# Layer 1 of a two-layer metaformer: rows' denominators inverted on ScalarE, five convolution taps on TensorE instead of seven, centred x kept in PSUM

## The chip, the cores and the metric

The kernel runs on one core of a Trainium2 chip. Its engines are named as in the profile: PE is TensorE (PEld its weight loads), DVE VectorE, ACT ScalarE, POOL GpSimd, SP the engine that issues the DMAs. Each works through its own queue of instructions strictly in order and waits by semaphores for the others. The metric is the device time of one execution in microseconds; lower is better.

## The reference, cut to what matters

The input x is 2 images of 96 channels by 96 x 96 pixels, fp32. Layer 0 (a selective-scan block and a feed-forward block) takes most of the time and isn't touched. Layer 1 is:

```python
    x = x + _L1_conv_ref(_ln_c(x), kv_w, q_w, lepe_w, lepe_b, proj_w, proj_b)
    t = _to_tokens(x)
    t = t + _L1_ffn_ref(_ln_t(t), W1, b1, W2, b2)
    x = _from_tokens(t, x)
...
def _ln_c(v, eps=1e-6):                       # over the 96 channels
    m = jnp.mean(v, axis=1, keepdims=True)
    s = jnp.var(v, axis=1, keepdims=True)
    return (v - m) / jnp.sqrt(s + eps)
...
def _L1_conv_ref(x, kv_w, q_w, lepe_w, lepe_b, proj_w, proj_b):
    k, v = jnp.split(kv, 2, axis=2)           # kv = kv_w x, three heads of 32
    x_samp = x.reshape(B, C, hh, R, ww, R).mean(axis=(3, 5))      # cells of 2 x 2 pixels
    q_samp = ...                              # q_w x_samp
    lepe = lax.conv_general_dilated(v, lepe_w, (1, 1), [(2, 2), (2, 2)],
                                    feature_group_count=C)        # 5 x 5, each channel alone
    attn = jax.nn.softmax(k^T q_samp * scale, axis=-2)
    distribution = v attn                     # 96 channels on 48 x 48 cells
    samp_unfold = unfold3(x_samp)             # each cell's 3 x 3 neighbours
    dmat = jax.nn.softmax(x_unfold . samp_unfold * C ** -0.5, axis=-1)
    feature = dmat . unfold3(distribution)    # each pixel: nine neighbouring cells, weighted
    out = feature + lepe
    return proj_w out + proj_b
```

(The einsums are written short here.) The feed-forward block is 96 to 384 to 96 with ReLU, its products in fp8 and its sums rounded to fp16. Its own norm is `_ln_t`, over the channels too, with eps 1e-5.

## The kernel before

The work is laid out with channels on partitions and pixels along the free dimension. A stripe is 6 rows of pixels, T = 576 columns; most instructions work on half of one, H2 = 288 columns.

Layer 1 goes through the two images one after the other, each in three stages.

1. **The norm for k, q, v** (`_l1_before`), 16 stripes. For each half stripe: PE multiplies x by (I - mean) into a PSUM tile `pc` (L1107), so `pc` is the centred x. ACT squares it into `sq` (L1112) and copies it to `xc` in SBUF (L1113). PE averages the squares into PSUM tile `va` (L1116). ACT turns that into 1/sqrt(va + eps) in place, as Ln (L780) and Exp with scale -0.5 (L781), in `_power`. DVE multiplies `xc` by `va` into `xn` (L1120). Then come the products with the weights of k, v and q, and their copies from PSUM on ACT.
2. **Attention** (`_l1_attention`): all pixels against all cells. It isn't touched. DVE adds the exponentials up there (L1425), PE makes scores (L1351) and weighted values (L1412).
3. **Rows** (`_l1_turn`, then `_l1_rows` for 8 groups of 12 pixel rows). For each group:
   - four matmuls and ACT copies bring v with a border of two pixels into `vch` (L1519, L1522);
   - `near`, three times: PE makes scores with the neighbouring cells (`st`, L1543), ACT takes Exp (L1547), POOL multiplies by a mask (L1549), PE sums the weights into `pd` and the weighted distribution into `po` (L1557), DVE inverts `pd` into `rd` (L1563) and multiplies `rd` by `po` into `ft` (L1564). All of these are 384 columns wide;
   - the 5 x 5 convolution: 25 taps. The taps listed in `ON_PE`, seven of them, are folded into the projection: PE multiplies a shifted view of `vch` by a projection matrix whose rows are scaled by the tap's weights (L1595; these matrices, `W.pt`, are built once ahead of layer 1). The other 18 are one DVE instruction each over 1152 columns that adds to `acc` (L1576 for the first, L1579 for the rest);
   - `project`: one PSUM tile `pp` for each half stripe gathers the taps on PE, then `ft` (L1599), then `acc` (L1605); DVE adds the bias and x (L1608);
   - `_plan_ffn`, the feed-forward block, which layer 0 uses as well: the norm once more (L794 centred, L799 Square, L800 copy to `xc`, L803 mean, `_power`, L807 the product as fp8), the hidden layer (L818, L821, L825, L828), the second product (L837, L841, L845) and the residual on POOL (L846).

What sets the order: the code of stages 1 and 3 only records operations, each with its engine, a cost, the tiles it reads and writes, and a due time. `_Plan.order` then places them one by one. It knows for every engine when it is free, for every tile how many buffers there are, and adds a fixed lag when one engine hands over to another; the earliest possible operation goes next, ties by due time. The order so found is fixed for each engine, so a DVE instruction that waits holds everything behind it in DVE's queue. PSUM is one pool of 8 buffers with a single tag, from which `pc`, `va`, `st`, `pd`, `po`, `pp`, the hidden layer and everything else in a stage take theirs. A buffer is free again after its tile's last user. A line of `_l1_rows` shows the form of a record, with the cost as a number of columns:

```python
        op("dve", 2200, lambda: nc.vector.reciprocal(rd.ap, pd.ap[:C, :384]), (pd,), (rd,))
        op("dve", 384, lambda: nc.vector.tensor_tensor(
            ft.ap[:, i], rd.ap, po.ap[:C, :384], ALU.mult), (rd, po), ((ft, i),))
```

The functions that the change touches:

Of the kernel before, what the change touches and what calls it, by code (L numbers as in the profile page):

```python
# [11 lines left out]
F8 = mybir.dt.float8e5  # L12
AF = mybir.ActivationFunctionType
ALU = mybir.AluOpType
# [11 lines left out]
C = 96  # L26
# [5 lines left out]
T = WIN * HW  # L32
H2 = T // 2
# [68 lines left out]
class _Plan:  # L102
# [15 lines left out]
    def op(self, eng, cost, run, r=(), w=(), due=0.0, tab=None, also=()):  # L118
        o = _Op(eng, cost, run, due, tab)
        ref = lambda t: t if isinstance(t, tuple) else (t, None)  # L120
        meets = lambda a, b: a is None or b is None or a == b
        for t, key in map(ref, r):
            o.deps.update(p for p, q in t.writes if meets(key, q))
        for t, key in map(ref, w):
            o.deps.update(p for p, q in t.writes + t.reads if meets(key, q))
        for t, key in map(ref, r):
            t.reads.append((o, key))
        for t, key in map(ref, w):
            t.writes.append((o, key))
        o.deps.discard(o)  # L130
        for t in [x[0] for x in map(ref, list(r) + list(w))] + list(also):
            if t not in o.tiles:
                o.tiles.append(t)
        for t in o.tiles:
            if not t.users and t.tag != "p":
                t.queue.append(t)
            t.users.append(o)
        self.ops.append(o)
        return o
# [632 lines left out]
        sofar += o.cost  # L772


def _power(k, op, v, eps):

    v_ = lambda: v.ap[:C, :H2]

    def run():
        k.nc.scalar.activation(v_(), v_(), AF.Ln, bias=eps[:C])  # L780
        k.nc.scalar.activation(v_(), v_(), AF.Exp, scale=-0.5)  # L781

    op("act", H2, run, (), (v,), tab="e", times=2)


def _plan_ffn(k, S, op, ps, temp, pool, bufs, ffn, x1):

    nc = k.nc
    cols = lambda c: slice(c * H2, (c + 1) * H2)
    xc, s1, xq = temp("fxc"), temp("fsq"), S.tile(pool, [C, T], "fxq", bufs, F8)  # L790
    for c in range(2):
        def norm(c=c):
            pc, va = ps("fxc"), ps("fva")
            op("pe", H2, lambda: nc.tensor.matmul(  # L794
                pc.ap[:C, :H2], k.less_mean, x1.ap[:, cols(c)], start=True, stop=True),
                (x1,), (pc,), (xc,))

            def centred():
                nc.scalar.activation(s1.ap[:, cols(c)], pc.ap[:C, :H2], AF.Square)  # L799
                nc.scalar.copy(xc.ap[:, cols(c)], pc.ap[:C, :H2])  # L800

            op("act", H2, centred, (pc,), ((xc, c), (s1, c)), times=2)
            op("pe", H2, lambda: nc.tensor.matmul(  # L803
                va.ap[:C, :H2], k.mean96, s1.ap[:, cols(c)], start=True, stop=True),
                ((s1, c),), (va,), (xq,))
            _power(k, op, va, k.eps5)
            op("dve", H2, lambda: nc.vector.tensor_tensor(  # L807
                xq.ap[:, cols(c)], xc.ap[:, cols(c)], va.ap[:C, :H2], ALU.mult, saturate=False),
                ((xc, c), va), ((xq, c),))

        norm()
    h16 = S.tile(pool, [128, NM, T], "fh16", bufs, HP)
    h8 = S.tile(pool, [128, NM, T], "fh8", bufs, F8)
    for m in range(NM):
        for c in range(2):
            def hidden(m=m, c=c):
                ph = ps("fph")
                op("pe", H2 // 2, lambda: nc.tensor.matmul(  # L818
                    ph.ap[:, :H2], ffn.w1[:, m * 128 : (m + 1) * 128], xq.ap[:, cols(c)],
                    start=True, stop=True), ((xq, c),), (ph,), (h16,))  # L820
                op("act", H2, lambda: nc.scalar.copy(h16.ap[:, m, cols(c)], ph.ap[:, :H2]),  # L821
                   (ph,), ((h16, m),))

            hidden()
        op("act", T, lambda m=m: nc.scalar.activation(  # L825
            h16.ap[:, m, :], h16.ap[:, m, :], AF.Relu, bias=ffn.b1[:, m : m + 1]),
            (), ((h16, m),))
        op("act", T, lambda m=m: nc.scalar.activation(  # L828
            h8.ap[:, m], h16.ap[:, m], AF.Copy, saturate=False), ((h16, m),), ((h8, m),))
    y16, x2 = S.tile(pool, [C, T], "fy16", bufs, HP), temp("x2")  # L830
    for c in range(2):
        def last(c=c):
            py = ps("fpy")

            def run():
                for m in range(NM):
                    nc.tensor.matmul(py.ap[:C, :H2], ffn.w2[:, m, :], h8.ap[:, m, cols(c)],  # L837
                                     start=(m == 0), stop=(m == NM - 1))

            op("pe", 3 * H2 // 2, run, (h8,), (py,), (y16,))  # L840
            op("act", H2, lambda: nc.scalar.copy(y16.ap[:, cols(c)], py.ap[:C, :H2]),  # L841
               (py,), ((y16, c),))

        last()
    op("act", T, lambda: nc.scalar.activation(y16.ap, y16.ap, AF.Identity, bias=ffn.b2), (), (y16,))  # L845
    op("pool", T, lambda: nc.gpsimd.tensor_tensor(x2.ap, x1.ap, y16.ap, ALU.add), (x1, y16), (x2,))  # L846
    return x2
# [242 lines left out]
def _l1_before(k, P, S, W, M, x2d):  # L1090


    nc = k.nc
    op = _op(S)
    ps = lambda name: S.tile(P.ps, [128, 512], "p", 8, name=name)
    cols = lambda c: slice(c * H2, (c + 1) * H2)
# [1 line left out]
    xn, xs, kH, qH, vT, mk, mq = map(held, ("xn", "xs", "kH", "qH", "vT", "mk", "mq"))  # L1098

    def stripe(s):  # L1100
        xt, xc, sq = (S.tile(P.wk, [C, T], n, 3, name="n" + n) for n in ("xt", "xc", "sq"))
        S.op("sp", 1.0, lambda: nc.sync.dma_start(xt.ap, x2d[:, s * T : (s + 1) * T]), (), (xt,))
        here = lambda c: slice(s * T + c * H2, s * T + (c + 1) * H2)

        def norm(c):
            pc, va = ps("nxc"), ps("nva")
            op("pe", H2, lambda: nc.tensor.matmul(  # L1107
                pc.ap[:C, :H2], k.less_mean, xt.ap[:, cols(c)], start=True, stop=True),
                (xt,), (pc,), (xc,))

            def centred():
                nc.scalar.activation(sq.ap[:, cols(c)], pc.ap[:C, :H2], AF.Square)  # L1112
                nc.scalar.copy(xc.ap[:, cols(c)], pc.ap[:C, :H2])  # L1113

            op("act", H2, centred, (pc,), ((xc, c), (sq, c)), times=2)
            op("pe", H2, lambda: nc.tensor.matmul(  # L1116
                va.ap[:C, :H2], k.mean96, sq.ap[:, cols(c)], start=True, stop=True),
                ((sq, c),), (va,))
            _power(k, op, va, k.eps6)
            op("dve", H2, lambda: nc.vector.tensor_tensor(  # L1120
                xn.ap[:, here(c)], xc.ap[:, cols(c)], va.ap[:C, :H2], ALU.mult),
                ((xc, c), va), ((xn, s),))
            pk = ps("pk")
            op("pe", H2, lambda: nc.tensor.matmul(  # L1124
                pk.ap[:C, :H2], W.k, xn.ap[:, here(c)], start=True, stop=True),
                ((xn, s),), (pk,))
            op("act", H2, lambda: nc.scalar.copy(kH.ap[:C, here(c)], pk.ap[:C, :H2]),
               (pk,), ((kH, s),))

        for c in range(2):  # L1130
            norm(c)
        for n, f in enumerate((ALU.max, ALU.min)):
            op("dve", T, lambda n=n, f=f: nc.vector.tensor_reduce(
                mk.ap[:, n, s : s + 1], kH.ap[:C, s * T : (s + 1) * T], AX.X, f),
                ((kH, s),), ((mk, (n, s)),))
        hs = S.tile(P.wk, [C, WIN, CELLS], "hs", 2)
        cells = lambda: xs.ap[:, 1 + 3 * s : 4 + 3 * s, 1 : CELLS + 1]

        def pairs():
            v = xn.ap[:, s * T : (s + 1) * T].rearrange("p (i w t) -> p i w t", w=CELLS, t=2)  # L1140
            nc.gpsimd.tensor_tensor(hs.ap, v[:, :, :, 0], v[:, :, :, 1], ALU.add)

        op("pool", H2, pairs, ((xn, s),), (hs,))
        op("pool", H2 // 2, lambda: nc.gpsimd.tensor_tensor(
            cells(), hs.ap[:, 0:6:2], hs.ap[:, 1:6:2], ALU.add), (hs,), ((xs, s),))
        op("pool", H2 // 2, lambda: nc.gpsimd.tensor_scalar(cells(), cells(), 0.25, None, ALU.mult),
           (), ((xs, s),))
# [336 lines left out]


NEAR = 2 * (CELLS + 2)
ON_PE = tuple(range(7))


def _l1_rows(k, P, S, W, ffn, M, distT, x2, out, q, at):  # L1490
# [43 lines left out]
    def near(i):  # L1534
# [25 lines left out]

        sums(pd, lambda t: k.ones[:NEAR])
        sums(po, lambda t: distT.ap[:NEAR, j + t])
        op("dve", 2200, lambda: nc.vector.reciprocal(rd.ap, pd.ap[:C, :384]), (pd,), (rd,))  # L1563
        op("dve", 384, lambda: nc.vector.tensor_tensor(  # L1564
            ft.ap[:, i], rd.ap, po.ap[:C, :384], ALU.mult), (rd, po), ((ft, i),))

# [17 lines left out]
    def project(c2):  # L1584
# [26 lines left out]

        for c in range(2):
            part(c)
        y = _plan_ffn(k, S, op, ps, temp, P.wk, 3, ffn, x3)
        row = q * R + c2 * WIN
        S.op("sp", 1.0, lambda: nc.sync.dma_start(
            out[:, row : row + WIN, :].rearrange("c r w -> c (r w)"), y.ap), (y,), ())
# [227 lines left out]
```

## Time and profile before

| | us |
|---|---|
| median of 3 runs | 9094.67 |
| lowest, highest | 9091.53, 9099.18 |
| layer 0 and the loading of layer 1's weights | about 6923 |
| norm for k, q, v, first and second image | 78 and 81 |
| attention, first and second image | 628 and 626 |
| rows, first and second image | 379 and 379 |

Over the whole span, PE is busy 7530.7 us (83%), DVE 8172.0 (90%), ACT 6380.3 (70%) and POOL 6182.8 (68%). These are averages over stages with different limits; the change lies in about a tenth of the span, so it is the stages' own busy times that count. In the views below, a line such as "rd<-pd 96x384 f32" means that tile `rd` was written from tile `pd`, 96 partitions by 384 elements. PE's fp32 products are two matmul instructions each in the profile.

### The profile page before, as it was taken

The page shows a single profiled execution, that of the slowest core. Times are in us where ns is not written, and L with a number is a line of the kernel's source. Part 1 is how long each engine was busy: PE and PEld are TensorE (multiplying, and loading weights), DVE is VectorE, ACT ScalarE, POOL GpSimd, SP SyncE. Part 2 cuts the span into 40 slices and gives each one's busy share as a digit, 9 for nine tenths or more (in the row PEclk, how much of TensorE's full clock was granted, in tenths as well). Part 3 has the DMA queues.
Part 4 walks back from the last instruction along what each step waited for, and adds up shares of the span by engine and source line. Part 5 has one row for each costly group of instructions (what it writes and reads, how often), then busy time and mean ns, then how long its engine had stood idle before and what let it go on. Part 6 is the DMA issues. An engine that isn't in the chain of part 4 may idle for free. (4 is left out here: it accounts for less than half of the span.)

```text
span 9094.2 us, 122612 instructions
## 1 busy us (share of the span) xinstructions
PE 7530.7 (83%) x43793; PEld 3599.2 (40%) x43793; DVE 8172.0 (90%) x5681; ACT 6380.3 (70%) x10752; POOL 6182.8 (68%) x3931
## 2 busy tenths in 40 slices
PE   6888888888788888888887888887857999989998
PEld 3333344443334344444343443343423334543345
DVE  2999999999999999999999999999996998959988
ACT  4677777777777777777777777777745785677755
POOL 4988888888888888888888988888863001310022
PEclk8889889898888888889898889888857999989999
DMA  2444444444444444444444444444431000000000
GB/s 81 134 145 140 140 143 140 139 139 140 139 138 142 139 143 143 138 139 145 138 137 141 141 136 143 144 136 144 142 122 36 2 2 7 23 25 2 3 11 21
DMA packets 335681, 969.61 MB, mean 107 GB/s; under 512 B 50424, under 2 KB 52144, under 8 KB 334768
## 3 DMA queue, kind: packets, MB, share of 16 engines
q1 hardware_dynamic: 335056, 961.64, 33.3%
q8 instruction: 348, 5.70, 0.3%
q14 instruction: 277, 2.27, 0.1%
HBM read 788.04 MB, written 132.17 MB: 101 GB/s over the span
## 5 line engine op out<-in xcount | busy, mean ns | idle before, releaser
L1018 POOL TENSOR_TENSOR h<-h,cre 128x864 f32<-128x864 f32 x2048 | 4121.7, 2021 | 824.2 <-DVE h L1015 405.4
L1015 DVE TENSOR_TENSOR_SCAN h<-dA,bp 128x864 f32<-128x864 f32 x2048 | 4001.7, 1954 | 250.3 <-DVE bp L1005 5.7
L991 ACT ACTIVATE dA<-dlr,A 128x576 f32<-128x576 f32 x3072 | 2156.9, 765 | 1223.4 <-DVE h L1015 1138.3
L1005 DVE TENSOR_TENSOR bp<-dur,B 128x864 f32<-128x864 f32 x2048 | 2176.4, 1063 | 249.1 <-DMA dur<-du_d 42.3
L1028 PE MATMUL y<-h,fold 128*32 128x288 f32 (+2 forms) x18432 | 1875.3, 453 | 111.0 <-POOL h L1018 107.7
L1002 PE MATMUL B<-bt,selb 128*128 128x288 bf16 x2048 | 637.8, 313 | 1105.7 <-DVE bp L1005 1098.1
L536 PE MATMUL pc<-xin,off 96*96 96x288 f32 x4608 | 1328.7, 416 | 0.9 <-ACT xin L501 0.9
L1028 PEld LDWEIGHTS y<-h,fold 128*32 128x32 f32 x18432 | 765.4, 120 | 1370.2 <-issue 647.8
L1355 ACT ACTIVATE pr<-sc 128x960 f32<-128x960 f32 (+1 forms) x1080 | 955.0, 936 | 257.9 <-DVE sums L1425 145.6
L1425 DVE TENSOR_TENSOR sums<-sums,pr 128x1920 f32<-128x1920 f32 (+1 forms) x510 | 1059.5, 2077 | 59.1 <-ACT pr L1355 7.0
L536 PEld LDWEIGHTS pc<-xin,off 96*96 96x96 f32 x4608 | 710.9, 165 | 622.7 <-issue 381.1
L1506 POOL MEMSET vch<- 96x32 f32 x16 | 2.0, 124 | 1328.6 <-DVE dist L1384 1266.2
L1351 PE MATMUL sc<-qH,kH 32*128 32x480 f32 (+1 forms) x3240 | 709.6, 602 | 10.1 <-DMA q<-qH 10.1
L1351 PE MATMUL sc<-q,kH 32*128 32x480 f32 (+1 forms) x1080 | 564.5, 602 | 0.0
L1412 PE MATMUL av<-pr,vT 128*32 128x480 f32 (+1 forms) x4320 | 533.5, 565 | 3.8 <-ACT av L1429 3.5
L1002 PEld LDWEIGHTS <-selb 128*128 128x128 bf16 x2048 | 201.6, 100 | 711.8 <-issue 636.6
L1351 PEld LDWEIGHTS sc<-qH,kH 32*128 32x128 f32 x3240 | 285.3, 185 | 439.2 <-issue 304.0
L1579 DVE SCALAR_TENSOR_TENSOR acc<-vch,lepe_w,acc 96x1152 f32<-96x1152 f32 x272 | 447.3, 1645 | 7.8
L709 PE MATMUL pt<-xd,w_dt 96*128 96x288 f32 x768 | 313.3, 500 | 25.9 <-ACT zs L519 12.9
L1549 POOL TENSOR_TENSOR e<-e,mask 100x384 f32<-100x384 f32 x96 | 151.9, 1603 | 223.2 <-ACT e L1547 223.2
L821 ACT CAST fh<-fph 128x288 f16<-128x288 f32 x384 | 141.2, 390 | 230.9 <-PE fph L818 229.5
L728 POOL TENSOR_TENSOR e<-e,du 128x576 f32<-128x576 f32 x192 | 271.1, 1412 | 25.2 <-ACT du L724 25.0
(258 smaller groups left out, 10550.5 us busy)
## 6 DMA issues: line engine op xcount, KB each, us to landing
cre<-c_d SPq DMA_DIRECT2D x1024, 288.0 KB
dur<-du_d SPq DMA_DIRECT2D x256, 864.0 KB
dlr<-dl_d SPq DMA_DIRECT2D x256, 864.0 KB
x<-xs SPq DMA_DIRECT2D x512, 72.0 KB
du_d<-du SPq DMA_DIRECT2D x128, 288.0 KB
dl_d<-dl SPq DMA_DIRECT2D x128, 288.0 KB
du_d<-du SPq DMA_DIRECT2D x128, 144.0 KB
dl_d<-dl SPq DMA_DIRECT2D x128, 144.0 KB
```

The costliest lines, as they stand in the source:

```text
L536: pe(H2, lambda: nc.tensor.matmul(pc.ap[:C, :H2], k.w_c1[:, ih, tap, oh * C : (oh + 1) * C], xin.ap[:, ih, 3 * c + dy : 3 * c + dy + 3, dx ...
L991: S.op("act", 0.76, lambda blk=blk: nc.scalar.activation(dA.ap[:, :, blk, :], dlr.ap[:, blk, :].rearrange("p (c n) -> p c n", c=2), AF.Exp ...
L1002: S.op("pe", 0.3, lambda: nc.tensor.matmul(pB.ap[:, :H2], k.selb[:, kk, i, :], f.bc[o].ap[:, toks], start=True, stop=True), (f.bc[o],), (p ...
L1005: S.op("dve", 1.13, lambda: nc.vector.tensor_tensor(bp.ap[:, : NBL * H2].rearrange("p (b n) -> p b n", b=NBL), dur.ap[:, :, toks], pB.ap[: ...
L1015: nc.vector.tensor_tensor_scan(hv, dv, bv, 0.0, ALU.mult, ALU.add)
L1018: S.op("pool", 2.06, lambda: nc.gpsimd.tensor_tensor(ht.ap, ht.ap, cre.ap[:, toks].unsqueeze(1).to_broadcast([128, NBL, H2]), ALU.mult), ( ...
L1028: nc.tensor.matmul(dst, k.fold, v, start=False, stop=stop)
L1351: nc.tensor.matmul(two[s // 2][:, s % 2, :n], kH[rows, k0 : k0 + 128], q, start=True, stop=True)
L1355: nc.scalar.activation(pr[:, 2 * i : 2 * i + 2, :n], two[i][:, :, :n], AF.Exp, scale=HD**-0.5)
L1412: nc.tensor.matmul((main if s < HEADS else other)[s * HD : (s + 1) * HD, :n], vT[:, blk, hd, :], pr[:, s, :n], start=at == 0, stop=at == e ...
L1425: nc.vector.tensor_tensor(sums[:, :, :n], sums[:, :, :n], pr[:, :, :n], ALU.add)
L1579: S.op("dve", 1.6, lambda: nc.vector.scalar_tensor_tensor(acc.ap, src(), W.lw[:, t : t + 1], acc.ap, ALU.mult, ALU.add), (vch,), (acc,))
```

## The change

It has three parts.

- In rows, the inverse of the denominators goes from DVE's reciprocal to ACT: Ln in place in PSUM and Exp with scale -1, as exp(-ln pd). It takes the slow reciprocals off DVE.
- `ON_PE` goes from seven taps to five, so DVE does 20 taps in place of 18 for each group and PE 5 in place of 7. It evens out what the first part frees.
- In the norm of stage 1 and in the feed-forward norm of rows (`roomy=True`; layer 0 keeps the old form), the copy of the centred x to SBUF is left out. `pc` stays in PSUM until DVE multiplies it, and Exp writes 1/sqrt to a new SBUF tile (`rs`, `frs`, 4 buffers) instead of back into `va`, since DVE's product then takes one operand from PSUM and one from SBUF as before.

```diff
-def _power(k, op, v, eps):
+def _power(k, op, v, eps, out=None):
...
-        k.nc.scalar.activation(v_(), v_(), AF.Exp, scale=-0.5)
+        k.nc.scalar.activation(v_() if out is None else out.ap, v_(), AF.Exp, scale=-0.5)
-    op("act", H2, run, (), (v,), tab="e", times=2)
+    op("act", H2, run, (), (v,) if out is None else (v, out), tab="e", times=2)
...
-def _plan_ffn(k, S, op, ps, temp, pool, bufs, ffn, x1):
+def _plan_ffn(k, S, op, ps, temp, pool, bufs, ffn, x1, roomy=False):
...
-    xc, s1, xq = temp("fxc"), temp("fsq"), S.tile(pool, [C, T], "fxq", bufs, F8)
+    xc = None if roomy else temp("fxc")
+    s1, xq = temp("fsq"), S.tile(pool, [C, T], "fxq", bufs, F8)
...
+            rs = S.tile(pool, [C, H2], "frs", 4) if roomy else None
...
                 nc.scalar.activation(s1.ap[:, cols(c)], pc.ap[:C, :H2], AF.Square)
-                nc.scalar.copy(xc.ap[:, cols(c)], pc.ap[:C, :H2])
+                if not roomy:
+                    nc.scalar.copy(xc.ap[:, cols(c)], pc.ap[:C, :H2])
...
-                xq.ap[:, cols(c)], xc.ap[:, cols(c)], va.ap[:C, :H2], ALU.mult, saturate=False),
-                ((xc, c), va), ((xq, c),))
+                xq.ap[:, cols(c)], pc.ap[:C, :H2] if roomy else xc.ap[:, cols(c)],
+                rs.ap if roomy else va.ap[:C, :H2], ALU.mult, saturate=False),
+                (pc, rs) if roomy else ((xc, c), va), ((xq, c),))
...
-            pc, va = ps("nxc"), ps("nva")
+            pc, va, rs = ps("nxc"), ps("nva"), S.tile(P.wk, [C, H2], "rs", 4)
...
-                nc.scalar.copy(xc.ap[:, cols(c)], pc.ap[:C, :H2])
...
-            _power(k, op, va, k.eps6)
+            _power(k, op, va, k.eps6, rs)
             op("dve", H2, lambda: nc.vector.tensor_tensor(
-                xn.ap[:, here(c)], xc.ap[:, cols(c)], va.ap[:C, :H2], ALU.mult),
-                ((xc, c), va), ((xn, s),))
+                xn.ap[:, here(c)], pc.ap[:C, :H2], rs.ap, ALU.mult), (pc, rs), ((xn, s),))
...
-ON_PE = tuple(range(7))
+ON_PE = tuple(range(5))
...
-        op("dve", 2200, lambda: nc.vector.reciprocal(rd.ap, pd.ap[:C, :384]), (pd,), (rd,))
+
+        def inverse():
+            nc.scalar.activation(pd.ap[:C, :384], pd.ap[:C, :384], AF.Ln)
+            nc.scalar.activation(rd.ap, pd.ap[:C, :384], AF.Exp, scale=-1.0)
+
+        op("act", 384, inverse, (), (pd, rd), tab="e", times=2)
...
-        y = _plan_ffn(k, S, op, ps, temp, P.wk, 3, ffn, x3)
+        y = _plan_ffn(k, S, op, ps, temp, P.wk, 3, ffn, x3, True)
```

More of the change, by code (lines that the diff above doesn't have):

```diff
@@ L793, in norm @@
             pc, va = ps("fxc"), ps("fva")
+            rs = S.tile(pool, [C, H2], "frs", 4) if roomy else None
             op("pe", H2, lambda: nc.tensor.matmul(
                 pc.ap[:C, :H2], k.less_mean, x1.ap[:, cols(c)], start=True, stop=True),
-                (x1,), (pc,), (xc,))
+                (x1,), (pc,), () if roomy else (xc,))
             def centred():
                 nc.scalar.activation(s1.ap[:, cols(c)], pc.ap[:C, :H2], AF.Square)
-                nc.scalar.copy(xc.ap[:, cols(c)], pc.ap[:C, :H2])
-            op("act", H2, centred, (pc,), ((xc, c), (s1, c)), times=2)
+                if not roomy:
+                    nc.scalar.copy(xc.ap[:, cols(c)], pc.ap[:C, :H2])
+            op("act", H2, centred, (pc,), ((s1, c),) if roomy else ((xc, c), (s1, c)),
+               times=1 if roomy else 2)
             op("pe", H2, lambda: nc.tensor.matmul(
@@ L805, in norm @@
                 ((s1, c),), (va,), (xq,))
-            _power(k, op, va, k.eps5)
+            _power(k, op, va, k.eps5, rs)
             op("dve", H2, lambda: nc.vector.tensor_tensor(
-                xq.ap[:, cols(c)], xc.ap[:, cols(c)], va.ap[:C, :H2], ALU.mult, saturate=False),
-                ((xc, c), va), ((xq, c),))
+                xq.ap[:, cols(c)], pc.ap[:C, :H2] if roomy else xc.ap[:, cols(c)],
+                rs.ap if roomy else va.ap[:C, :H2], ALU.mult, saturate=False),
+                (pc, rs) if roomy else ((xc, c), va), ((xq, c),))
         norm()
@@ L1100, in stripe @@
     def stripe(s):
-        xt, xc, sq = (S.tile(P.wk, [C, T], n, 3, name="n" + n) for n in ("xt", "xc", "sq"))
+        xt, sq = (S.tile(P.wk, [C, T], n, 3, name="n" + n) for n in ("xt", "sq"))
         S.op("sp", 1.0, lambda: nc.sync.dma_start(xt.ap, x2d[:, s * T : (s + 1) * T]), (), (xt,))
@@ L1105, in norm @@
         def norm(c):
-            pc, va = ps("nxc"), ps("nva")
+            pc, va, rs = ps("nxc"), ps("nva"), S.tile(P.wk, [C, H2], "rs", 4)
             op("pe", H2, lambda: nc.tensor.matmul(
                 pc.ap[:C, :H2], k.less_mean, xt.ap[:, cols(c)], start=True, stop=True),
-                (xt,), (pc,), (xc,))
-            def centred():
-                nc.scalar.activation(sq.ap[:, cols(c)], pc.ap[:C, :H2], AF.Square)
-                nc.scalar.copy(xc.ap[:, cols(c)], pc.ap[:C, :H2])
-            op("act", H2, centred, (pc,), ((xc, c), (sq, c)), times=2)
+                (xt,), (pc,))
+            op("act", H2, lambda: nc.scalar.activation(
+                sq.ap[:, cols(c)], pc.ap[:C, :H2], AF.Square), (pc,), ((sq, c),))
             op("pe", H2, lambda: nc.tensor.matmul(
```

## The prediction

> **What bounds the kernel now.** I read three things in this order: the stretches of the kernel with each engine's busy time, the chain that ended last inside the stretches that the change touches, and then the groups of instructions there.
>
> The first view is the table of windows. Columns: the stretch, its length, and busy time with number of instructions for PE, PEld, DVE, ACT and POOL, then the granted clock, the DMA share and GB/s. The two long rows are the "rows" stage of each image, the two short ones the norm for k, q and v.
>
> ```profile
> core 0: us, PE busy (x) PEld busy (x) DVE busy (x) ACT busy (x) POOL busy (x), PEclk, DMA share, GB/s
> 6923.00:7001.00 78.00, 70.97 (x352) 50.49 (x352) 41.75 (x81) 65.97 (x187) 31.66 (x50) 0.96 0.19 49
> 7629.00:8008.00 379.00, 339.88 (x1273) 203.05 (x1273) 325.38 (x257) 207.30 (x454) 112.67 (x84) 0.91 0.07 19
> 8008.00:8089.00 81.00, 70.92 (x350) 50.53 (x350) 41.59 (x80) 65.98 (x187) 27.37 (x48) 0.92 0.21 56
> 8715.00:9094.00 379.00, 339.78 (x1273) 203.11 (x1273) 324.78 (x257) 207.09 (x454) 111.20 (x82) 0.91 0.07 19
> ...
> 8739.00:9052.00 313.00, 290.15 (x1099) 173.39 (x1098) 306.97 (x240) 169.41 (x377) 97.77 (x67) 0.95 0.07 20
> 9052.00:9094.00 42.00, 26.10 (x99) 15.92 (x97) 3.60 (x8) 25.88 (x55) 3.81 (x3) 0.74 0.06 16
> ```
>
> The change reaches only these 917 us. In rows, DVE is busy 325 of 379 us; inside the middle 313 us it is busy 307 (98%), and before and after it there is a head of 24 us and a tail of 42 us. PE is close behind with 290 of 313 (93%), ACT is at 54%.
>
> Whether DVE or PE binds, the chain and DVE's waits say. First line: the chain from 8715 to the end. Last two: all that DVE waited for from 8724 to 9050.
>
> ```profile
> by line: DVE acc L1579 49.2%; DVE rd L1563 11.8%; PE pp L1595 6.6%; issue 3.3%; DVE x L1608 3.1%; DVE fxq L807 2.4%; PE pv L1519 2.2%; PE st L1543 2.1%; PE pd L1557 2.1%; DVE ft L1564 2.1%; PE po L1557 1.8%; DVE acc L1576 1.5%; PE fph L818
> ```
> ```profile
> DVE acc L1576 <- ACT vch L1522: 9.4, 1, 9.4
> DVE rd L1563 <- PE pd L1557: 0.3, 1, 0.3
> ```
>
> Two lines of DVE, the taps (L1579) and the reciprocals (L1563), carry 61% of the chain, and after the first vch DVE waits for practically nothing. So rows is DVE-bound between its head and tail. The groups of rows in the first image give the prices (busy us, mean ns of one, then idle before):
>
> ```profile
> L1579 DVE SCALAR_TENSOR_TENSOR acc<-vch,lepe_w,acc 96x1152 f32<-96x1152 f32 x136 | 224.1, 1648 | 3.9
> L1595 PE MATMUL pp<-vch,pt 96*96 96x288 f32 x448 | 119.3, 419 | 0.3 <-DVE ft L1564 0.3
> L1549 POOL TENSOR_TENSOR e<-e,mask 100x384 f32<-100x384 f32 x48 | 75.0, 1583 | 106.7 <-ACT e L1547 106.7
> L1563 DVE RECIPROCAL rd<-pd 96x384 f32<-96x384 f32 x24 | 61.1, 2545 | 0.3 <-PE pd L1557 0.3
> L1547 ACT ACTIVATE e<-st 100x384 f32<-100x384 f32 x48 | 22.0, 493 | 17.8 <-PE st L1543 17.8
> L800 ACT COPY fxc<-fxc 96x288 f32<-96x288 f32 x32 | 12.5, 391 | 0.0
> ```
> ```profile
> L1579 DVE SCALAR_TENSOR_TENSOR acc<-vch,lepe_w,acc x272: 1398/1415/4227, 7639.4 to 9050.2; 96x1152 f32<-96x1152 f32 x136
> L1563 DVE RECIPROCAL rd<-pd x48: 2540/2545/2554, 7646.9 to 9043.6; 96x384 f32<-96x384 f32 x48
> ```
>
> The last two lines (min/median/max) matter: the reciprocal always takes 2.54 us, a tap 1.415 us in the median but 1.648 in the mean and up to 4.2. Something disturbs the taps and not the reciprocals.
>
> **What the Trainium skill says.** (1) "SBUF — State Buffer", Who interferes with whom: a DVE instruction with two SBUF inputs contends with a GpSimd instruction that reads SBUF, and one with at most one SBUF input doesn't. The tap reads vch and acc from SBUF, the reciprocal only PSUM; the spread above agrees. (2) "ScalarE: Activation LUTs", What ACT_TABLE_LOAD costs: with immediate scale and bias an activation takes 186 ns + 0.833 N, an estimate of 506 ns at N=384. The trace's Exp of 384 columns takes 493 ns, and I use that. (3) "Perfetto Trace Analysis", Identifying the Most-Contended Engine: matmul busy share is no measure of how full PE is. I therefore lean on DVE's waits, not on PE's 93%.
>
> **The change part by part**, per image; times two at the end.
>
> Reciprocals leave DVE: 24 x 2.545 = 61.1 us, all in the dense middle.
>
> Two taps come back to DVE: 8 passes x 2 = 16 taps. At the undisturbed 1.415 they cost 22.6 us. The disturbance: 224.1 - 136 x 1.415 = 31.7 us were lost to POOL now, while taps filled 224/325 = 69% of DVE's busy time and the reciprocals, where POOL works unhindered, 19%. POOL's work is unchanged. With the reciprocals gone taps fill about 86%, so the loss scales to 31.7 x 86/69 = 39.5, 7.8 us more. The two ends are 22.6 (no more collisions) and 30.4 us; I take 30.4, since POOL has nowhere else to go. Net for DVE: 61.1 - 30.4 = 30.7 us saved (38.5 at the other end).
>
> TensorE: 32 groups of pp x 2 taps x 2 passes = 128 matmuls fewer of 448. At 119.3/448 = 0.266 us that is 34 us less, so PE falls by as much as DVE and doesn't become the bound: about 306 of 346. In the tail the tap matmuls lie on the end's chain: there the chain has three runs of 14 taking 6.14, 3.40 and 3.40 us, each of which becomes 10, saving 4/14 of 12.9 = 3.7 us. I count 3.
>
> ACT: Ln and Exp on 384 columns, 24 x 2 x 0.493 = 23.7 us, less the copies of xc, 12.5 us: 207 becomes 218 of 346, 63%. That hides under DVE. It puts a wait where none was: ft (L1564) had its reciprocal just ahead on DVE, now it waits for ACT. ACT's queue holds runs of hidden-layer work ahead of an inverse, as 3 x (2 x 0.394 + 0.775 + 0.683) = 6.7 us. Behind a stalled ft lie the taps of the same quarter, and behind these the projection. Against this, the order moves ft behind one or more taps, and Ln plus Exp (1.0 us) is ready sooner than the 2.5 us reciprocal. I count 1 us, with 0 and 24 (1 us for each ft) as ends.
>
> Rows together: 30.7 + 3 - 1 = about 33 us per image, 379 to 346. The head of 24 us (transposes, first values and scores) isn't touched.
>
> The norm for k, q, v: 32 copies of 0.41 us leave ACT, 66 to 53 us in 78. But PE is busy 71 of the 78, and in mid-stage its matmuls follow each other without waits, so PE hides nearly all of it. I count 1 us per image; ends -2 (worse, see below) and 8. pc now keeps one of the eight PSUM buffers from its first matmul until DVE's product, while va is free earlier, after Exp instead of after the product.
>
> The building of five instead of seven scaled matrices sits before the first norm while PE waits for a load (lb from DRAM 8.9 us): nothing. Layer 0 and attention have the same instructions in the same order: nothing.
>
> Sum: 2 x (33 + 1) = 68 us. 9094.67 - 68 = about 9027 us.
>
> **Rivals.**
> B: ft waits for ACT. For: ACT's 6.7 us runs, the in-order queues, and only 6 us of DVE slack in 313 now. Against: most of the inverses stand ahead of such a run. With 1 us per ft, 24 x 2 = 48 us come back, of which I counted 2: 9027 + 46 = 9073.
> C: PSUM becomes the bound. pc is held through Square, a matmul, Ln, Exp and the product, in both stages, and PE cannot run ahead. A wait of 2 us for each of the 16 stripes of a norm stage and each of the 16 feed-forward tiles of rows would be 2 x 32 x 2 = 128 us, so 9027 + 128 = 9155, slower. Against: va gives its buffer back earlier, and PE waits now for DVE (fxq), hardly for buffers.
> D: more than counted. ACT is back to back in the middle of the norm stage (66 of 78), so it, not PE, could set that stage; then the 13 us come out whole, and the taps collide no more than now (38.5): 2 x (38.5 + 3 + 8) = 99 us, 9094.67 - 99 = 8996.
>
> **How the numbers follow.** A (9027) 0.66, B 0.18, C 0.04, D 0.12. The predicted time is A's. The range runs from 9003 (most of the way to D) to 9057 (nearly two thirds of B's waits), which leaves out about 2 in 10. Faster by over 0.2% means under 9076.5: A, D and most of B, 0.93. Within 0.2%: the worst of B and the mildest of C, 0.04. Slower: 0.03.
>
> **What would show each step right or wrong.** Right: rows about 346 us per image with DVE busy near 295; no reciprocal in rows; 152 taps at a mean of about 1.67 us with a median still near 1.415; pp taps down to 320 matmuls; ACT near 218; DVE's waits in the middle under 10 us; the norm stage still 76 to 79 us with PE about 71. Wrong: ft waiting for ACT by tens of us (B), PE idle before fxc or nxc for a buffer (C), the norm stage down by 5 us or more, or taps at a mean of 1.6 (D). A granted PE clock well under 0.91 in rows would shift all of it.

## The result and the profile after

The changed kernel takes 9015.41 us (median of 4 runs, 9009.51 to 9021.88) against 9094.85 us before; the ratio is 0.9913, 95% interval 0.9895 to 0.993. That is 79 us less, where 68 us less were forecast. The profiled run of the changed kernel (9021.88 us, its profile spans 9020.1) was the slowest of the four. The totals below come from several rounds, in which the kernel before took 9094.3 to 9097.5 us in the median, so a difference of 3 us between two of them means nothing.

Stage by stage, from the start of one to the start of the next in the two profiles:

| us | before | after | difference |
|---|---|---|---|
| layer 0 | 6923.9 | 6933.3 | +9.4 |
| norm for k, q, v | 80.2, 80.5 | 78.9, 78.2 | -1.3, -2.3 |
| attention | 625.0, 623.5 | 624.9, 625.3 | -0.1, +1.8 |
| rows | 382.2, 378.8 | 340.1, 339.4 | -42.1, -39.4 |

Layer 0 has the same instructions in the same order in both. Over the profiles of all the kernels below, in which it is the same too, it took 6924.7 to 6931.1 us, and the two profiles here happen to be its ends; so I take the +9.4 for its spread from run to run, not for the change. The norm stages and rows together give 85 us in these profiles.

The windows of rows in the second image: the whole stage, its middle (from the first tap to the end of the last one), and the tail after that. First the kernel before, then the changed one; columns as in the prediction (PE, PEld, DVE, ACT, POOL, clock, DMA).

```profile
8715.44:9094.20 378.76, 339.78 (x1273) 203.08 (x1273) 324.48 (x256) 207.09 (x454) 111.20 (x82) 0.91 0.07 19
8724.74:9051.65 326.91, 304.04 (x1142) 180.25 (x1141) 320.88 (x248) 176.28 (x390) 106.70 (x72) 0.95 0.07 19
9051.65:9094.20 42.55, 26.45 (x100) 16.07 (x98) 3.60 (x8) 26.20 (x56) 3.81 (x3) 0.74 0.06 16
```
```profile
8680.66:9020.10 339.44, 299.01 (x1145) 176.10 (x1145) 289.17 (x248) 219.03 (x470) 113.56 (x82) 0.94 0.08 21
8688.35:8981.30 292.95, 270.61 (x1024) 157.44 (x1023) 284.65 (x238) 185.61 (x400) 109.05 (x72) 0.97 0.07 21
8981.30:9020.10 38.80, 20.71 (x88) 12.51 (x86) 4.51 (x10) 28.79 (x61) 3.81 (x3) 0.79 0.07 21
```

The middle fell by 34.0 us, DVE's busy time in it by 36.2. DVE is still busy 97% of it and PE 92%: the bound hasn't moved. The tail fell by 3.8 us. One thing besides has changed: the granted clock of TensorE over the stage went from 0.91 to 0.94.

The groups of rows in the first image of the changed kernel that answer to those shown before (busy us, mean ns of one):

```profile
L1585 DVE SCALAR_TENSOR_TENSOR acc<-vch,lepe_w,acc 96x1152 f32<-96x1152 f32 x152 | 246.3, 1620 | 3.8
L1550 POOL TENSOR_TENSOR e<-e,mask 100x384 f32<-100x384 f32 x48 | 86.9, 1832 | 81.2 <-ACT e L1548 81.1
L1601 PE MATMUL pp<-vch,pt 96*96 96x288 f32 x320 | 83.2, 405 | 1.7 <-DVE ft L1570 1.1 <-ACT fh L827 0.6
L1570 DVE TENSOR_TENSOR ft<-rd,po 96x384 f32<-96x384 f32 x24 | 12.8, 541 | 0.0
```

The reciprocals (61.1 us) are gone, and DVE sat idle 0.0 us before ft. 16 more taps cost 246.3 - 224.1 = 22.2 us. The mask's multiplication on GpSimd went from 1583 to 1832 ns each: we come back to that. The tap that starts each group has an instruction of its own, which takes 0.81 us when nothing disturbs it. It grew too; in the second image, before and after:

```profile
L1576 DVE TENSOR_SCALAR acc<-vch,lepe_w 96x1152 f32<-96x1152 f32 x8 | 6.9, 864 | 9.4 <-ACT vch L1522 9.4
L1582 DVE TENSOR_SCALAR acc<-vch,lepe_w 96x1152 f32<-96x1152 f32 x8 | 12.1, 1514 | 8.0 <-ACT vch L1523 7.8
```

All that DVE waited for in the middle of the second image, in three lines:

```profile
DVE acc L1582 <- ACT vch L1523: 7.8, 1, 7.8
DVE x L1614 <- PE pp L1611: 3.8, 4, 1.4
DVE fxq L812 <- ACT frs L781: 0.6, 1, 0.6
```

(The first is the head of the stage, just at the window's edge.) ft and the inverse don't appear. The chain through the stage is more mixed than it was:

```profile
by line: DVE acc L1585 34.3%; PE pp L1601 11.3%; issue 8.3%; POOL e L1550 5.6%; PE pv L1520 3.0%; ACT fh L831 2.8%; PE po L1558 2.5%; PE pd L1558 2.3%; PE pp L1611 2.2%; ACT fh L834 2.2%; ACT fh L827 2.2%; PE pp L1605 2.1%; DVE x L1614 2.0%
```

### The profile page after: what moved, and what is told of

Its sections match the earlier page's. It is cut to its first block, busy times and chain, and to the rows that moved or that the text cites. A ratio compares the mean times of both kernels' runs of the same rounds, so it can differ in the third digit from the quotient of the medians.

```text
span 9020.1 us, 122080 instructions
## 1 busy us (share of the span) xinstructions
PE 7473.2 (83%) x43537; PEld 3552.9 (39%) x43537; DVE 8098.6 (90%) x5663; ACT 6393.2 (71%) x10720; POOL 6194.7 (69%) x3931
## 4 chain that ended last, share of the span: by engine, by line
DVE 39%; PE 14%; issue 3%; ACT 2%; POOL 1%; DVEq 1%; DMA 0%; SPq 0%; POOLq 0%; ACTq 0%
DVE h L1021 19%; DVE bp L1011 11%; DVE sums L1426 6%; PE sc L1352 4%; DVE acc L1585 3%; PE av L1413 3%; PE y L1034 1%; PE pp L1601 1%; PE pd L669 0%; PE nxc L1113 0%; POOL e L1550 0%; DVEq L1021 0%; PE pk L1125 0%; PE px L608 0%; PE pv L1157 0%
## 5 line engine op out<-in xcount | busy, mean ns | idle before, releaser
L1585 DVE SCALAR_TENSOR_TENSOR acc<-vch,lepe_w,acc 96x1152 f32<-96x1152 f32 x304 | 489.9, 1612 | 7.6
L1550 POOL TENSOR_TENSOR e<-e,mask 100x384 f32<-100x384 f32 x96 | 171.5, 1808 | 175.6 <-ACT e L1548 175.3
L730 POOL TENSOR_TENSOR dl<-dl,r 128x576 f32<-128x576 f32 x192 | 270.2, 1407 | 6.2
```

The lines of the kernel that those rows point to most:

```text
L1585: S.op("dve", 1.6, lambda: nc.vector.scalar_tensor_tensor(acc.ap, src(), W.lw[:, t : t + 1], acc.ap, ALU.mult, ALU.add), (vch,), (acc,))
```

## The experiments

Because layer 0 spreads by several us, the time of rows in the profile says more than the total. For each: the median in all, rows of both images together, and for the second image the middle, the tail, and how much of the middle DVE and PE were busy; then what the taps lost in both images, that is their busy time less 1.415 us each, the undisturbed median. Each kernel has one profile; attention, the same in all of them, takes 623.5 to 625.6 us in them, which says how far a stage spreads.

| kernel | total | rows | middle | tail | DVE, PE | taps lost |
|---|---|---|---|---|---|---|
| before | 9094.9 | 761.0 | 326.9 | 42.5 | 98%, 93% | 62.4 |
| changed | 9015.4 | 679.5 | 293.0 | 38.8 | 97%, 92% | 59.7 |
| 1 inverse only | 9038.5 | 704.3 | 293.1 | 47.6 | 89%, 97% | 63.0 |
| 2 taps only | 9121.7 | 783.4 | 349.9 | 32.1 | 98%, 88% | 66.8 |
| 3 norm only | 9094.1 | 760.0 | 329.6 | 39.3 | 98%, 93% | 63.4 |
| 4 inverse and taps | 9025.8 | 691.1 | 290.6 | 44.6 | 97%, 92% | 62.6 |
| 5 changed, six taps | 9031.5 | 702.4 | 299.6 | 41.4 | 91%, 93% | 64.9 |
| 6 changed, four taps | 9022.1 | 690.2 | 303.4 | 32.8 | 98%, 89% | 70.8 |
| 7 changed, no mask | 8983.6 | 649.3 | 267.6 | 46.9 | 97%, 97% | 18.2 |
| 8 changed, idle copy | 9029.6 | 696.8 | 297.8 | 42.9 | 96%, 92% | 59.3 |
| 9 mask on PE | 8975.4 | 639.4 | 268.9 | 41.6 | 96%, 98% | 15.5 |
| 10 mask on PE, four taps | 8975.9 | 638.8 | 279.1 | 32.5 | 97%, 95% | 19.1 |
| 11 changed, other order | 9023.8 | 688.5 | 290.9 | 44.6 | 97%, 94% | 62.6 |
| 12 as 4, mask's cost of 11 | 9027.1 | 688.7 | 290.4 | 42.0 | 98%, 92% | 59.7 |

The last column leaves out the first tap of each group. These lost another 8.0 us in the changed kernel, 7.7 in kernel 8, 6.6 in 12, 4.4 in 4 and at most 2.0 in the others. With them the loss is 62.5 to 70.8 us in the kernels with the mask on GpSimd and 17.5 to 19.1 us in the other three.

### One part at a time

**1, the inverse alone.** The kernel before with

```diff
-        op("dve", 2200, lambda: nc.vector.reciprocal(rd.ap, pd.ap[:C, :384]), (pd,), (rd,))
+        def inverse():                                              # Ln, then Exp with scale -1
...
+        op("act", 384, inverse, (), (pd, rd), tab="e", times=2)
```

> Only the inverse on ScalarE; seven taps on TensorE and the copies of centred x as before. Theory 1 (DVE's busy time sets rows until TensorE's does): DVE loses 61 us per image, TensorE keeps 340 us of work in a stage that took 379, 290 of it in a middle of 313 us, so TensorE becomes the bound and rows ends near 355 us: about 9045 us in all (9035 to 9060). Theory 2 (DVE alone matters, TensorE has room): rows falls by the 61 us, about 8975. Theory 3 (the added work and waits of ScalarE cost something that the copies' removal pays for): ft waits for ScalarE and the time stays above 9060.

Ratio 0.9939 (0.9925 to 0.9952), 9038.5 us. The middle and tail of its second image:

```profile
8697.25:8990.32 293.07, 284.27 (x1112) 171.04 (x1110) 259.59 (x222) 191.52 (x422) 108.75 (x71) 0.99 0.07 20
8990.32:9037.90 47.58, 31.27 (x128) 19.44 (x128) 5.14 (x11) 32.57 (x72) 5.08 (x4) 0.80 0.07 19
```

Theory 1 holds: DVE sheds its 61 us, but rows falls by 28 us per image, since PE is now busy 97% of the middle and DVE 89%. DVE's waits there name PE, and ScalarE too, which itself waits there mainly for PE (for `pd` alone 35.4 us):

```profile
DVE fxq L807 <- ACT fva L781: 10.0, 8, 3.8
DVE x L1613 <- PE pp L1610: 8.5, 3, 7.6
DVE ft L1569 <- PE po L1557: 2.5, 1, 2.5
```

PE also has more left over when DVE is through, and the tail grows by 5 us.

**2, the taps alone.**

```diff
-ON_PE = tuple(range(7))
+ON_PE = tuple(range(5))
```

> Only five taps on TensorE instead of seven; reciprocals on DVE, copies as before. Theory 1 (DVE-bound): 16 taps more per image at 1.4 to 1.65 us, 22 to 26 us per image less about 3 us in the tail, about 9134 us (9125 to 9145). Theory 2 (TensorE was the bound): not slower, 9095 or less.

9121.7 us, ratio 1.003 (1.0018 to 1.0043): slower, as DVE's bound has it, but by 27 us rather than 39, below the range of 9125 to 9145. The middle did grow as reckoned, by 23.0 us; the tail shrank by 10.4 us, from 42.5 to 32.1, instead of 3.

**3, the norms alone.** The changed kernel with the reciprocal and seven taps.

> Only the norms without the copy of centred x, in the stage for k, q, v and in rows; reciprocals on DVE, seven taps on TensorE. Theory 1 (ScalarE isn't the bound): the norm stages give the 1.3 and 2.3 us that the changed kernel shows there, rows nothing: about 9091 us (9085 to 9096). Theory 3 (ScalarE's relief matters in rows as well): 9080 or less.

9094.1 us, ratio 0.9998 (0.9989 to 1.0006): no difference that can be measured. Its norm stages took 78.5 and 78.0 us, as in the changed kernel, and rows 1 us less over both images.

**4, inverse and taps, without the norms.**

> The changed kernel but for the norms, which keep their copies of centred x: the inverse on ScalarE and five taps on TensorE. Theory 1: all of the gain in rows is here and only the norm stages' 3.6 us are missing, about 9019 us (9010 to 9026). Theory 3 (with the copies ScalarE has 231 us of work in rows, and the inverses queue behind it): ft waits for ScalarE by 10 us per image or more, 9035 us or more.

9025.8 us, ratio 0.9926 (0.9913 to 0.994), at the upper end of theory 1's range. In rows the inverse alone gives 56.7 us, the taps alone cost 22.4, together they give 69.9. DVE waits for ft in neither image by more than 1 us. But 11.6 us of rows' gain are still missing beside the changed kernel, more than theory 1 allows, and in the second image they lie in the tail (44.6 against 38.8 us), not in the middle (290.6 against 293.0).

### What the norms' part is worth in rows

**8, an idle copy.** The changed kernel with ScalarE's copy put back in the feed-forward norm:

```diff
-    xc = None if roomy else temp("fxc")
+    xc = temp("fxc")
...
-                if not roomy:
-                    nc.scalar.copy(xc.ap[:, cols(c)], pc.ap[:C, :H2])
+                nc.scalar.copy(xc.ap[:, cols(c)], pc.ap[:C, :H2])
```

> The changed kernel with the copy of centred x to SBUF put back into the feed-forward norm of rows, but with nobody reading it: ScalarE does the work, the product still takes pc from PSUM. Theory A (what the norm's part gave in rows is ScalarE's time, by 12.5 us per image): the tail grows back to 45 to 47 us, rows to 343 to 347 us, about 9023 in all. Theory B (what counts is which buffers are held and the order that follows): the tail stays near 39 to 41 us and the time within 4 us of 9015.

9029.6 us, ratio 0.9923 (0.9909 to 0.9936). The total speaks for theory A rather than B, though not cleanly: the tail of the second image is 42.9 us, under A's 45 to 47, and about half of that image's loss lies in the middle, of which A says nothing. The copy changes the order as well, so two more kernels ask for the order's share.

**11, only the order.** The changed kernel, its instructions the same, with one planned cost corrected:

```diff
-                op("pool", 384, lambda: nc.gpsimd.tensor_tensor(
+                op("pool", 730, lambda: nc.gpsimd.tensor_tensor(
                     e[t].ap, e[t].ap, W.mask[:, t], ALU.mult), (), (e[t],))
```

> The changed kernel with nothing but the planned cost of the mask's multiplication changed, from 1.0 us to the 1.8 us that it takes on the chip; the instructions are the same, their order may differ. Theory (rows is bound by DVE's busy time, the waits in its middle are under 6 us): within 6 us of the changed kernel's 9015. Rival (an order made with wrong costs is what leaves the tail): the tail falls below 36 us and the time below 9005.

9023.8 us, ratio 0.992 (0.9907 to 0.9934): 8 us slower than the changed kernel, against both expectations. The middle is as good (290.9 us), the tail is not:

```profile
8690.39:8981.28 290.89, 272.15 (x1005) 159.57 (x1003) 282.73 (x238) 183.70 (x396) 109.29 (x71) 0.95 0.07 20
8981.28:9025.90 44.62, 27.67 (x106) 16.25 (x106) 4.78 (x10) 30.84 (x66) 5.09 (x4) 0.75 0.07 20
```

Beside the changed kernel's tail, PE has 106 matmuls left instead of 88. So with the same work in another order rows is 4 to 5 us longer per image. The granted clock went with it. Over the whole stage of the second image:

```profile
8681.11:9025.90 344.79, 309.10 (x1145) 182.59 (x1145) 287.50 (x248) 219.15 (x470) 115.07 (x82) 0.91 0.07 21
```

The same 1145 matmuls kept PE busy 309.1 us at a clock of 0.91 here and 299.0 us at 0.94 in the changed kernel. Whether the order costs time by itself, or through the clock, or whether the clock differed for another reason, isn't separated. Chance it hardly is: the five totals of kernel 11 all lie above the four of the changed kernel.

**12, the copies in that order.** Kernel 4 with the same corrected cost.

> The inverse on ScalarE and five taps, copies of centred x kept (as in the fourth experiment), and the mask's planned cost at 1.8 us (as in the eleventh). Theory A (the 12.5 us of copies on ScalarE lengthen rows): 4 to 8 us per image longer than the eleventh, 9032 to 9040 in all. Theory B (the tail is a matter of the order that comes out, and the copies are hidden): rows within 3 us of the eleventh's 344 us or shorter, so at most 9029 with the norm stages' 3 us.

9027.1 us, ratio 0.9922 (0.9908 to 0.9935). Rows takes 688.7 us against 688.5 in kernel 11, with 12.5 us more of copies per image on ScalarE. That is as theory B has it: in this pair the copies cost nothing that shows. The same planned cost doesn't give both the same order, though, so this pair too differs in more than the copies.

```profile
8693.48:8983.92 290.44, 266.49 (x1007) 155.86 (x1006) 283.88 (x238) 192.31 (x428) 106.51 (x72) 0.97 0.07 21
8983.92:9025.90 41.98, 26.01 (x107) 15.84 (x105) 4.59 (x10) 30.12 (x65) 3.81 (x3) 0.74 0.06 16
```

Four pairs of kernels with and without the copies, then, give 1 us (before and 3), 11.6 us (4 and changed), 17.3 us (8 and changed) and 0.2 us (12 and 11), and the same work in another order differs by 9 us in rows (changed and 11). What the norms' part gives is about 3 us in the norm stages: both together take 158.8 to 160.7 us in the five kernels with the copies there and 156.5 to 157.3 in the nine without. That it gives anything in rows beyond the order that happens to come out isn't shown.

### Five taps, or another number

**5 and 6**: six and four taps on TensorE in the changed kernel.

> The changed kernel with six taps on TensorE. Theory 1 (the middle of rows is DVE's, busy 97% there, with TensorE at 92%; the tail after the last tap is work left over for TensorE and ScalarE): the middle loses up to 13 us of DVE but TensorE gains 17 us, so it stops near 287 us, and the tail grows by about 4 us as it does with seven taps; rows ends within 4 us of the changed kernel's 340 us, 9008 to 9024 in all. Rival (DVE alone matters): rows 327 us, about 8990.

> The changed kernel with four taps on TensorE. Theory 1: 8 more taps per image at 1.6 us lengthen the middle by 13 us, the tail shrinks by 3 to 4 us: rows 349 us, about 9034 us in all. Rival (TensorE binds): the middle falls with its 17 us and the time is under 9010.

Six: 9031.5 us, ratio 0.9929 (0.9916 to 0.9943), above both expectations. The middle was to stop near 287 us and took 299.6, with neither engine busy over 93%. DVE's waits there name two long ones for the norm's ScalarE work and a second one for vch, which the changed kernel doesn't have:

```profile
DVE acc L1582 <- ACT vch L1523: 14.6, 2, 7.6
DVE fxq L812 <- ACT frs L781: 12.3, 2, 6.6
```

That looks like an unlucky order once more; no run with another order of six taps was made, so it stays open. Four: 9022.1 us, ratio 0.9918 (0.9904 to 0.9931), faster than expected. The middle grew by 10.4 us and the tail fell by 6.0. By rows it is 10.7 us slower than five, hardly more than another order is worth, and the intervals of the two ratios overlap. Five is the best of the three in the order that each came out with; that it is the best number as such isn't shown.

### Why the two taps were cheaper than forecast

The forecast had the taps lose more to GpSimd as they fill more of DVE's time. The table's last column says otherwise: 59 to 71 us in every kernel with the mask on GpSimd, before the change and after. Kernel 1 tests the scaling itself. It has as many taps as the kernel before, and they fill 84% of DVE's busy time in place of 69%; they lost 63.0 us, with the first taps of each group, against 63.2.

**7, no mask.**

```diff
-                op("pool", 384, lambda: nc.gpsimd.tensor_tensor(
-                    e[t].ap, e[t].ap, W.mask[:, t], ALU.mult), (), (e[t],))
```

> The changed kernel without the multiplication of e by the mask on GpSimd, so the sums take in cells that aren't neighbours. Theory (a GpSimd instruction that reads SBUF delays one tap, whatever else DVE does; 128 such instructions cost 60 to 67 us of taps in every kernel so far, 0.49 us each): with the 32 residual additions alone the taps lose 16 us in both images and their mean falls from 1.61 to about 1.47 us; DVE is 22 us less busy per image and rows falls by 8 to 18 us, as TensorE's 270 us of the middle come to bind. Rival (the taps are slow for another reason, such as TensorE's or ScalarE's traffic): their mean stays above 1.57 us.

The kernel leaves the mask out, so it computes something else; it is there for its time alone. 8983.6 us, ratio 0.9876 (0.9861 to 0.9891). The taps in both images:

```profile
L1583 DVE SCALAR_TENSOR_TENSOR acc<-vch,lepe_w,acc 96x1152 f32<-96x1152 f32 x304 | 448.4, 1475 | 7.2
```

A mean of 1475 ns, as foretold; the loss falls to 18.2 us. The mask's 96 multiplications, then, cost these taps 59.7 - 18.2 = 41.5 us, 0.43 us each. The first taps of the groups are undisturbed here, which is another 8.0 us. The 18.2 us that stay are put down to the 32 residual additions; no run was made without those. The middle falls by 25 us, until PE is as full as DVE (97% each).

### A version that beats both

**9, the mask on TensorE.** With GpSimd's multiplication shown to cost DVE 25 us per image (first taps included), the mask goes into the scores ahead of Exp, as a large negative number. The scores' own matmul no longer closes its group, and the pair's planned cost is 480:

```diff
+                    nc.tensor.matmul(
+                        st.ap[:NEAR, :384], W.idb, W.neg[:, t], start=False, stop=True)
...
-                op("pool", 384, lambda: nc.gpsimd.tensor_tensor(
-                    e[t].ap, e[t].ap, W.mask[:, t], ALU.mult), (), (e[t],))
...
+        W.neg = cp.tile([NEAR, 2, 384], BF, tag="neg", name="neg")
+        nc.vector.tensor_scalar(W.neg, W.mask, 30000.0, -30000.0, ALU.mult, ALU.add)
+        W.idb = cp.tile([NEAR, NEAR], BF, tag="idb", name="idb")
+        nc.vector.tensor_copy(W.idb, k.ident[:NEAR, :NEAR])
```

> The changed kernel with the mask laid on the scores by TensorE: a bf16 matmul of the identity with 0 and -30000 adds into st ahead of Exp, and the multiplication on GpSimd is gone. Five taps on TensorE. Theory: DVE as without the mask (taps at 1.47 us, 264 us busy per image), TensorE 48 x 2 / 2 = 48 short matmuls more per image, about 8 us: the middle 268 to 278 us, rows 326 to 336, about 8995 us in all (8985 to 9008). Rival (TensorE is so full without the mask, 260 of 267 us, that the new matmuls and their loads come on top twice over): 9010 or more.

8975.4 us (8972.55 to 8977.48), ratio 0.9868 (0.9853 to 0.9883): below its range, and about 40 us less than the changed kernel. Stage, middle and tail of the second image:

```profile
8653.25:8970.70 317.45, 295.61 (x1193) 179.87 (x1193) 264.11 (x248) 217.76 (x470) 28.52 (x34) 0.97 0.08 23
8660.20:8929.08 268.88, 264.55 (x1058) 159.49 (x1057) 259.42 (x238) 182.99 (x397) 22.74 (x23) 1.00 0.08 21
8929.08:8970.70 41.62, 24.12 (x103) 14.74 (x101) 4.69 (x10) 30.25 (x65) 5.08 (x4) 0.80 0.08 26
```

PE is busy 98% of the middle and DVE 96%. The middle was as expected (268 to 278 us); the tail came out 5 us shorter than without any mask, which nothing had foretold.

**10, the same with four taps on TensorE.**

> The same with four taps on TensorE: TensorE loses 17 us per image, DVE gains 8 taps at 1.45 us, 12 us. Theory: DVE binds again at 271 of a middle of about 279 us, the tail is shorter (near 40 us): rows 328 us, within 8 us of the version with five taps, 8985 to 9003. Rival (TensorE binds both): clearly faster than with five, by 15 us or more.

8975.9 us (8967.67 to 8981.16), ratio 0.9868 (0.9852 to 0.9883), below its range: the middle is 279.1 us, as expected, but the tail 32.5 rather than 40. What DVE loses in the middle comes back in the tail, and the two versions are even.

## Why the prediction was right, point by point

- *Only norm stages and rows change.* Right: attention moved by under 2 us, layer 0 within its own spread.
- *DVE bounds rows between head and tail.* Right. Taps alone made the kernel slower, and in the changed kernel DVE is busy 97% of the middle.
- *61.1 us of reciprocals leave DVE.* Right, and kernel 1 shows that they would not have come out whole without the second part: PE stops rows at 28 us less per image. The taps' move, which by itself costs 22.4 us over both images, adds 13.2 us to the inverse's 56.7 (kernels 1 and 4).
- *Two taps cost 30.4 us on DVE.* Mis-sized. The 22.6 us of undisturbed taps were right, but of the 7.8 us of further collisions only 1.5 us came in the first image and 3.2 in the second, as the first taps of the groups grew by 2.0 and 5.2 us and the others lost a little less than before. DVE's busy time fell by 37.0 and 35.3 us, not by 30.7. The wrong step was to scale the loss by the taps' share of DVE's time (kernel 1). Where the collisions that didn't come went isn't shown. GpSimd's mask and residual took 227.3 us over both images against 216.4 before, and PE waited for the mask 6 to 9 times an image, up to 1.2 us; but in kernel 4, with as many taps, GpSimd took 209.5. This term is the main part of the 8 us per image by which rows beat its forecast. The end named as rival D (38.5 us saved on DVE, taps at a mean of 1.6) was the one nearer the truth: the mean is 1.61.
- *The tail gives 3 us, as runs of 14 tap matmuls become 10.* 3.7 us in each image: the number was right by luck, the reason too small a part. The same instructions in kernel 11's order have a tail 2 us longer than before. With five taps the tail ran from 32 to 45 us: 32.1 in kernel 2, 38.8 in the changed kernel, 44.6 in kernels 4 and 11. It holds what PE and ACT still have to do when DVE is through, and depends on which engine runs ahead and on the order.
- *Waits of ft for ACT, 1 us.* Right: none in the changed kernel. Rival B didn't happen.
- *PE doesn't become the bound, ACT ends near 218 us.* Right: 299 and 219 us of 340. PE lost 41 us rather than 34: its tap group fell by 36, and the rest goes with the higher granted clock, 0.94 against 0.91. PE's busy share, which the prediction distrusted, was a good guide in this case: it had PE busy 290 of 313 us, and without the reciprocals alone (kernel 1) the middle stops at 293 us with PE busy 97% of it.
- *The norm stage gives 1 us, PE hides the copies' end.* Right: 1.3 and 2.3 us. PE stayed at 71 us. ACT went from 66 to 60, not 53: the prediction took off whole durations of copies, but consecutive instructions of ACT overlap in the trace (its groups add up to 80.9 us there before, and it was busy 66.0). Rival C, waits for PSUM, isn't to be seen in either stage. Rival D speaks of 13 us here and counts 8 in its sum; neither came.

The order that came out is part of the result: kernel 11's would have given 71 us in place of 79, nearer to the 68 foretold. The prediction said nothing of the order, so 8 us of where it landed are luck.

## What to carry to other kernels

Where two engines are near the limit of a stage, moving work off one gives only the distance to the other: price both parts together, and look for the part that evens them out. Split a stage into the middle, where the bound runs without a gap, and the tail after its last instruction; a balance that lengthens one shortens the other. When a planner fixes the order, make the same work run in a second order before crediting a small part of a change: here another order, with the clock that came with it, was worth 9 us.

## What the runs showed of the hardware

The Trainium skill, "SBUF — State Buffer", Summary: rules for kernel authors, says that where a DVE instruction has two SBUF inputs and a GpSimd instruction reads SBUF, the second one to issue waits until the first is through. Kernel 7 agrees in that taps get shorter without GpSimd's multiplications. What was new here is the price in a stage: with the first taps of the groups, taps lost 62 to 71 us in all kernels with 128 such GpSimd instructions and 17 to 19 us with 32, about half a microsecond for each. Whether taps filled 69% of DVE's busy time (before) or 84% (kernel 1) made no difference.

The first tap of a group has only one tile of pixels to read beside its weights, and GpSimd held it up as well. In the changed kernel it took 0.81 us at least and 3.52 at most; all that were longer than 0.82 us overlapped a GpSimd multiplication or addition, and without the mask none was longer.

A bf16 matmul of 384 columns that adds the mask to fp32 scores in the same PSUM group took 0.33 us by the trace, 15.7 us for the 48 of an image. That didn't show in PE's total: in the second image's rows PE was busy 295.6 us with them (kernel 9) and 298.0 without (kernel 7). But the granted clock was 0.97 in the one and 0.94 in the other, so this is no price for them:

```profile
8659.21:8983.00 323.79, 298.03 (x1145) 177.37 (x1145) 263.87 (x248) 217.16 (x470) 27.18 (x34) 0.94 0.08 23
```
